# Channel-norm statistics: one instruction over two interleaved groups of 128 values

## The chip, the cores and the metric

The kernel runs on one core of a Trainium2 chip. The metric is the device time of one execution in microseconds (us), lower is better. Times of a kernel are compared by the median of several runs. The engines are PE (matmuls), PEld (its weight loads), DVE (VectorE), ACT (ScalarE), POOL (GpSimd) and SP (SyncE, which issues transfers here).

## The reference

The input is x of shape (4, 128, 128, 128): 4 images of 128 channels and 128 x 128 pixels, all float32. Two layers follow each other, each added to its input.

Layer 0 works on tokens, which are pixels with 128 channels. The input goes through a group norm, then through this block:

```python
t = _ln(t, ln0_g, ln0_b)
y1 = _ln(t, ln1_g, ln1_b)
att = jnp.einsum('btc,oc->bto', jax.nn.sigmoid(y1) * y1, W_out)
t = t + att
y2 = _ln(t, ln2_g, ln2_b)
wht = jnp.einsum('btc,oc->bto', y2, W_whiten)
k = jnp.square(jax.nn.relu(jnp.einsum('btc,hc->bth', wht, W_key)))
kv = jnp.einsum('bth,ch->btc', k, W_value)
r = jax.nn.sigmoid(jnp.einsum('btc,oc->bto', wht, W_recep))
t = t + r * kv
```

`_ln` subtracts the mean over the 128 channels of a token and multiplies by 1/sqrt(variance + 1e-5). The reference runs the block also on the transposed image and adds both, which is twice the same, as the block treats each token by itself.

Layer 1 is a group norm, a 3 x 3 convolution of 128 to 128 channels, a bias and a gate per channel.

The three calls of `_ln` are the channel norms that this change is about.

## The kernel before, in words

**Tiling.** An image is cut into 16 pairs of two halves. A half is 512 tokens, that is SUB = 4 groups of 128 tokens. So there are 64 pairs over the four images. PE transposes a half (`ut`, line L659) so that 128 tokens lie on the partitions and the channels in a row; a half is then a tile of 128 partitions x 4 groups x 128 channels.

**A norm of a pair.** For norm k (0, 1 or 2) and pair g, the following steps are made:

- `bn` (L690): for each half, four DVE instructions, one for each group. Each reads 128 contiguous values of every partition and writes six numbers. The instruction keeps the elements at even places and those at odd places apart: for each of the two it gives a count, a mean and a sum of squared deviations. So a token's 128 channels come out as two halves of 64, which have to be joined. Norm 0 reads `ut` in PSUM; norms 1 and 2 read `t` in SBUF.
- `norm_start` (L707 to L713): joins the two sets for the pair's 8 groups at once, on tiles of 128 x 8: the difference of the means, its square, a scaling with epsilon added, the sum of the two spreads, the total, and (norms 0 and 1) the sum of the means.
- `norm_root` (L718): the power -1/2 on POOL.
- `norm_end` (L724, L725), norms 0 and 1 only: halves the sum of means (with its sign turned) and multiplies it by the root, which gives the bias of the normalisation.

For the first two pairs (EARLY) `norm_start` and `norm_end` run on DVE, for all others on POOL.

**Who uses it.** Norms 0 and 1: ACT applies scale and bias (L666), eight instructions for a pair. After norm 0 POOL multiplies by the gain (L742) and adds the shift (L746). After norm 1 PE transposes back, ACT makes the SiLU (L757), PE multiplies by W_out (`att`, L763), and DVE adds the result to `t` (L767). Norm 2: DVE transposes the four rows of the tile `four` (L775), of which only the first is used; SP writes it to memory (L781) and reads it back spread over all partitions as `R` (L786), and DVE multiplies the transposed `t` by it (L799). This is the input of the key matmuls (`pk`, L810), whose results go through ACT (L814, L820) into the value matmuls (`kv`, L837). DVE and POOL add the outcome to the image (L847, L853, L857), and DVE takes statistics of it for layer 1 (L863). DVE also reads the images to come for their group norm (L1004).

**The convolution** of an image runs beside layer 0 of the next ones: DVE prepares sums of rows (L899 to L937), PE multiplies (`m`, L875 to L877), ACT and DVE put the rows together (L951 to L973).

**Order.** Each engine works through its queue in order, and the order is written out by hand in lists (FILL, FIRST, HANDOVER, ORDER, BOUND, END), from which the program issues one step after the other. The change leaves the lists as they are.

Of the kernel before, what the change touches and what calls it, by code (L numbers as in the profile page):

```python
# [9 lines left out]
F32 = mybir.dt.float32  # L10
AF = mybir.ActivationFunctionType
ALU = mybir.AluOpType

P = 128
CH = 512
SUB = CH // P
# [3 lines left out]
LN_EPS = 1e-5  # L20
# [261 lines left out]
def conv_preact_kernel(  # L282
# [40 lines left out]
    nc = tc.nc  # L323
    B, C, H, W = x.shape
# [8 lines left out]
    N = PAIR * SUB  # L333
# [7 lines left out]
    small = ctx.enter_context(tc.tile_pool(name="small", bufs=4))  # L341
# [67 lines left out]
    nhalf = const.tile([P, N], F32, tag="nhalf", name="nhalf")  # L409
# [233 lines left out]
    S = {}  # L643
# [38 lines left out]
    def norm_source(k, g, h):  # L682
        return S["ut", g, h] if k == 0 else S["t", g][:, h]

    def bn(k, g, h):
        if ("st", k, g) not in S:
            S["st", k, g] = small.tile([P, N, 6], F32, tag=f"st{k}", name="st", bufs=2)
        st, src = S["st", k, g], norm_source(k, g, h)
        for s in range(SUB):
            nc.vector.bn_stats(st[:, h * SUB + s, :], src[:, s, :])  # L690

    def norm_start(k, g, eng):

        st = S.pop(("st", k, g))

        def term(name):
            return small.tile([P, N], F32, tag=f"{name}{k}", name=name, bufs=2)

        if k < 2:
            rs, nb, sm = term("rs"), term("nb"), term("sm")
            d, dd = rs, rs
        else:
            S["turn", g] = four = small.tile([P, 4, N], F32, tag="four", name="four", bufs=2)
            rs, nb, sm, dd, d = four[:, 0], None, four[:, 1], four[:, 2], four[:, 3]
        eng.tensor_tensor(d, st[:, :, 1], st[:, :, 4], ALU.subtract)  # L707
        eng.tensor_tensor(dd, d, d, ALU.mult)
        eng.tensor_scalar(dd, dd, C / 4, C * LN_EPS, ALU.mult, ALU.add)
        eng.tensor_tensor(sm, st[:, :, 2], st[:, :, 5], ALU.add)  # L710
        eng.tensor_tensor(rs, dd, sm, ALU.add)  # L711
        if k < 2:
            eng.tensor_tensor(sm, st[:, :, 1], st[:, :, 4], ALU.add)  # L713
        S["terms", k, g] = rs, nb, sm

    def norm_root(k, g):
        rs, _, _ = S["terms", k, g]
        nc.gpsimd.tensor_tensor(rs, rs, nhalf, ALU.pow)  # L718

    def norm_end(k, g, eng):  # L720
        rs, nb, sm = S.pop(("terms", k, g))
        S["norm", k, g] = rs, nb
        if k < 2:
            eng.tensor_tensor(sm, sm, nhalf, ALU.mult)  # L724
            eng.tensor_tensor(nb, sm, rs, ALU.mult)  # L725

    def norm_terms(k, g):
        if g < EARLY:
            norm_end(k, g, nc.vector)
        else:  # L730
            norm_start(k, g, nc.gpsimd)
            norm_root(k, g)
            norm_end(k, g, nc.gpsimd)
# [274 lines left out]
    def layer0_op(op, g):  # L1008
# [4 lines left out]
            "u": lambda: lay(g, *d),  # L1013
            "Tu": lambda: lay_turned(g, *d),
            "bn": lambda: bn(d[0], g, d[1]),
            "sa": lambda: norm_start(d[0], g, nc.vector),
            "pw": lambda: norm_root(d[0], g),
            "nb": lambda: norm_terms(d[0], g),
            "t": lambda: first_norm(g, *d),
# [166 lines left out]
```

## Time and profile before

| what | value |
|---|---|
| median of 3 runs | 1869.69 us (1868.83 to 1871.25) |
| span of the profiled execution | 1871.1 us |
| PE busy | 1806.3 us (97%) |
| DVE busy | 1348.0 us (72%) |
| ACT busy | 1269.8 us (68%) |
| POOL busy | 1164.7 us (62%) |
| statistics of the norms (L690) | 219.0 us from SBUF, 112.3 us from PSUM |
| roots on POOL (L718) | 215.4 us for norms 0 and 1, 105.0 us for norm 2 |

The page gives one time for the profiled execution, its span from the first to the last instruction; the times of the runs stand beside it in a list of their own. A group of instructions is told by line, engine, operation, what it writes and reads, how often, its busy time and the mean of one in ns, and by the idle time of the engine just before it with what ended most of it. Durations of successive DVE instructions overlap, so the busy time of a group is less than count times mean. The granted clock of PE was 0.996 on the mean.

### The profile page before, as it was taken

The page shows a single profiled execution, that of the slowest core. Times are in us where ns is not written, and L with a number is a line of the kernel's source. Part 1 is how long each engine was busy: PE and PEld are TensorE (multiplying, and loading weights), DVE is VectorE, ACT ScalarE, POOL GpSimd, SP SyncE. Part 2 cuts the span into 40 slices and gives each one's busy share as a digit, 9 for nine tenths or more (in the row PEclk, how much of TensorE's full clock was granted, in tenths as well). Part 3 has the DMA queues.
Part 4 walks back from the last instruction along what each step waited for, and adds up shares of the span by engine and source line. Part 5 has one row for each costly group of instructions (what it writes and reads, how often), then busy time and mean ns, then how long its engine had stood idle before and what let it go on. Part 6 is the DMA issues. An engine that isn't in the chain of part 4 may idle for free.

```text
span 1871.1 us, 21825 instructions
## 1 busy us (share of the span) xinstructions
PE 1806.3 (97%) x6096; PEld 942.6 (50%) x6096; DVE 1348.0 (72%) x3336; ACT 1269.8 (68%) x2493; POOL 1164.7 (62%) x1915
## 2 busy tenths in 40 slices
PE   3799999999999999999999999999999999999999
PEld 2555555555545555455455455455455555554443
DVE  6767766677677677777757677777766667676987
ACT  2889899898666776777667777677766777753000
POOL 2878888887366666886556666788555667641211
PEclk9899999999999999999999999999999999999999
DMA  5211112221212212222112212211201111111112
GB/s 219 89 46 57 46 49 96 73 71 58 71 59 85 91 68 103 84 87 96 42 68 91 77 50 77 75 63 68 81 12 68 68 57 68 50 39 45 52 68 90
DMA packets 46072, 133.57 MB, mean 71 GB/s; under 512 B 8679, under 2 KB 15102, under 8 KB 38014
## 3 DMA queue, kind: packets, MB, share of 16 engines
q1 hardware_dynamic: 45504, 131.77, 20.5%
q8 instruction: 49, 0.80, 0.2%
q14 instruction: 73, 0.60, 0.1%
q10 hardware_dynamic: 446, 0.40, 0.1%
HBM read 97.14 MB, written 35.00 MB: 71 GB/s over the span
## 4 chain that ended last, share of the span: by engine, by line
PE 84%; DVE 5%; POOL 5%; DMA 3%; ACT 2%; issue 1%; SPq 0%; DVEq 0%; POOLq 0%
PE kv L837 21%; PE pk L810 21%; PE m L875 8%; PE m L877 8%; PE m L876 8%; PE pr L828 5%; PE att L763 5%; PE tt L659 3%; PE ut L659 3%; PE z1t L659 3%; DMA x<-in_x 1%; POOL rs L718 1%; DMA R<-rd 1%; DVE st L690 1%; ACT t L666 1%
## 5 line engine op out<-in xcount | busy, mean ns | idle before, releaser
L810 PE MATMUL pk<-y,wk_s 128*128 128x512 f32 x1024 | 503.3, 594 | 1.6 <-ACT h L814 0.9
L837 PE MATMUL kv<-h,wv 128*128 128x512 f32 x1024 | 492.7, 593 | 0.0
L814 ACT ACTIVATE h<-pk,kbias 128x512 f32<-128x512 f32 x512 | 349.3, 687 | 188.1 <-PE pk L810 178.3
L857 POOL TENSOR_TENSOR x<-x,r 128x512 f32<-128x512 f32 x128 | 166.7, 1302 | 202.4 <-DVE r L853 193.2
L837 PEld LDWEIGHTS kv<-h,wv 128*128 128x128 f32 x1024 | 187.1, 190 | 201.9 <-issue 177.2
L820 ACT ACTIVATE h<-h 128x512 f32<-128x512 f32 x480 | 286.5, 629 | 3.4
L810 PEld LDWEIGHTS pk<-y,wk_s 128*128 128x128 f32 x1024 | 183.0, 191 | 185.2 <-issue 148.0
L666 ACT ACTIVATE t<-ut,nb,rs 128x128 f32<-128x128 f32 x512 | 191.4, 466 | 90.6 <-POOL nb L725 82.7
L690 DVE BATCH_NORM_STATS2 st<-t 128x6 f32<-128x128 f32 x1024 | 219.0, 278 | 30.5 <-POOL t L746 28.7
L666 ACT ACTIVATE z<-t,nb,rs 128x128 f32<-128x128 f32 x512 | 209.5, 489 | 17.5 <-POOL nb L725 17.1
L718 POOL TENSOR_TENSOR rs<-rs,nhalf 128x8 f32<-128x8 f32 x128 | 215.4, 1682 | 6.0 <-DVE rs L711 6.0
L742 POOL TENSOR_TENSOR t<-t,g 128x512 f32<-128x512 f32 x128 | 163.8, 1285 | 74.7 <-ACT t L666 74.3
L875 PE MATMUL m<-v,u 128*128 128x512 f32 x384 | 198.5, 598 | 10.4 <-DVE v L899 5.0
L877 PE MATMUL m<-v,u 128*128 128x508 f32 x384 | 195.7, 591 | 0.0
L876 PE MATMUL m<-v,u 128*128 128x508 f32 x384 | 195.5, 591 | 0.0
L746 POOL TENSOR_TENSOR t<-t,b 128x512 f32<-128x512 f32 x128 | 166.0, 1304 | 5.6
L853 DVE SCALAR_TENSOR_TENSOR r<-r,kv 128x512 f32<-128x512 f32 x128 | 87.0, 680 | 86.2 <-PE kv L837 83.4
L763 PEld LDWEIGHTS att<-wo,y 128*128 128x128 f32 x1024 | 131.9, 196 | 31.5 <-issue 22.4
L767 DVE TENSOR_TENSOR t<-att,t 128x512 f32<-128x512 f32 x128 | 87.7, 685 | 78.3 <-PE att L763 77.8
L690 DVE BATCH_NORM_STATS2 st<-ut 128x6 f32<-128x128 f32 x512 | 112.3, 283 | 40.4 <-PE ut L659 39.8
L763 PE MATMUL att<-wo,y 128*128 128x128 f32 x1024 | 138.0, 280 | 0.8 <-DVE t L767 0.4
L828 PE MATMUL pr<-y,wr_s 128*128 128x512 f32 x256 | 130.7, 594 | 0.9 <-DVE h L824 0.7
(164 smaller groups left out, 2491.2 us busy)
## 6 DMA issues: line engine op xcount, KB each, us to landing
R<-rd SPq DMA_DIRECT2D x128, 256.0 KB
x<-in_x SPq DMA_DIRECT2D x31, 1024.0 KB
out<-x SPq DMA_DIRECT2D x31, 1024.0 KB
xs<-in_x SPq DMA_DIRECT2D x48, 512.0 KB
rd<-rrow SPq DMA_DIRECT2D x256, 1.0 KB
u<-raw SPq DMA_DIRECT2D x18, 192.0 KB
raw<-u SPq DMA_DIRECT2D x6, 192.0 KB
x<-in_x SPq DMA_DIRECT2D x2, 512.0 KB
```

What stands on the lines that cost most here:

```text
L666: nc.scalar.activation(dst[:, s, :], src[:, s, :], AF.Identity, bias=nb[:, i : i + 1], scale=rs[:, i : i + 1],)
L690: nc.vector.bn_stats(st[:, h * SUB + s, :], src[:, s, :])
L718: nc.gpsimd.tensor_tensor(rs, rs, nhalf, ALU.pow)
L763: nc.tensor.matmul(att[:, ts(s, P)], y[:, ts(s, P)], wo, start=True, stop=True)
L810: nc.tensor.matmul(pk, wk_s[:, ts(j, P)], S["y2", g, h], start=True, stop=True)
L814: nc.scalar.activation(k, S["pk", g, h, j], AF.Relu, bias=kbias[:, j : j + 1])
L820: nc.scalar.activation(k, k, AF.Square)
L828: nc.tensor.matmul(pr, wr_s, S["y2", g, h], start=True, stop=True)
L837: nc.tensor.matmul(S["kv", g, h], wv[:, j, :], S.pop(("h", g, h, j)), start=(j == 0), stop=(j == NH - 1))
L875: nc.tensor.matmul(pc, u[:, 1], v, start=True, stop=False)
L876: nc.tensor.matmul(pc[:, :, 1:W], u[:, 0], v[:, :, 0 : W - 1], start=False, stop=False)
L877: nc.tensor.matmul(pc[:, :, 0 : W - 1], u[:, 2], v[:, :, 1:W], start=False, stop=True)
```

## The change

A statistics instruction now reads two groups of 128 in alternation: element 0 of the first group, element 0 of the second, element 1 of the first and so on. The elements at even places are then those of one group and the elements at odd places those of the other, so that the six numbers are the two groups' own count, mean and spread. A half takes two such instructions of 256 elements instead of four of 128. The joining goes: `norm_start` only adds epsilon to the spread and turns the sign of the mean, and `norm_end` is one product. For norm 2 the one operation of `norm_start` fills all four rows of `four`.

```diff
     def bn(k, g, h):
         if ("st", k, g) not in S:
-            S["st", k, g] = small.tile([P, N, 6], F32, tag=f"st{k}", name="st", bufs=2)
+            S["st", k, g] = small.tile([P, N, 3], F32, tag=f"st{k}", name="st", bufs=2)
         st, src = S["st", k, g], norm_source(k, g, h)
-        for s in range(SUB):
-            nc.vector.bn_stats(st[:, h * SUB + s, :], src[:, s, :])
+        for s in range(0, SUB, 2):
+            i = h * SUB + s
+            two = src[:, s : s + 2, :].rearrange("p s c -> p c s")
+            nc.vector.bn_stats(st[:, i : i + 2, :].rearrange("p n f -> p (n f)"), two)
...
         if k < 2:
-            rs, nb, sm = term("rs"), term("nb"), term("sm")
-            d, dd = rs, rs
+            rs, nb = term("rs"), term("nb")
+            eng.tensor_scalar(rs, spread, C * LN_EPS, None, ALU.add)
+            eng.tensor_scalar(nb, mean, -1.0, None, ALU.mult)
         else:
             S["turn", g] = four = small.tile([P, 4, N], F32, tag="four", name="four", bufs=2)
-            rs, nb, sm, dd, d = four[:, 0], None, four[:, 1], four[:, 2], four[:, 3]
-        eng.tensor_tensor(d, st[:, :, 1], st[:, :, 4], ALU.subtract)
-        eng.tensor_tensor(dd, d, d, ALU.mult)
-        eng.tensor_scalar(dd, dd, C / 4, C * LN_EPS, ALU.mult, ALU.add)
-        eng.tensor_tensor(sm, st[:, :, 2], st[:, :, 5], ALU.add)
-        eng.tensor_tensor(rs, dd, sm, ALU.add)
-        if k < 2:
-            eng.tensor_tensor(sm, st[:, :, 1], st[:, :, 4], ALU.add)
-        S["terms", k, g] = rs, nb, sm
+            rs, nb = four[:, 0], None
+            eng.tensor_scalar(
+                four, st[:, :, 2:3].rearrange("p n f -> p f n").to_broadcast([P, 4, N]),
+                C * LN_EPS, None, ALU.add,
+            )
+        S["terms", k, g] = rs, nb
...
         if k < 2:
-            eng.tensor_tensor(sm, sm, nhalf, ALU.mult)
-            eng.tensor_tensor(nb, sm, rs, ALU.mult)
+            eng.tensor_tensor(nb, nb, rs, ALU.mult)
```

More of the change, by code (lines that the diff above doesn't have):

```diff
@@ L686, in bn @@
         if ("st", k, g) not in S:
-            S["st", k, g] = small.tile([P, N, 6], F32, tag=f"st{k}", name="st", bufs=2)
+            S["st", k, g] = small.tile([P, N, 3], F32, tag=f"st{k}", name="st", bufs=2)
         st, src = S["st", k, g], norm_source(k, g, h)
-        for s in range(SUB):
-            nc.vector.bn_stats(st[:, h * SUB + s, :], src[:, s, :])
+        for s in range(0, SUB, 2):
+            i = h * SUB + s
+            two = src[:, s : s + 2, :].rearrange("p s c -> p c s")
+            nc.vector.bn_stats(st[:, i : i + 2, :].rearrange("p n f -> p (n f)"), two)
     def norm_start(k, g, eng):
         st = S.pop(("st", k, g))
+        mean, spread = st[:, :, 1], st[:, :, 2]
         def term(name):
@@ L701, in norm_start @@
         if k < 2:
-            rs, nb, sm = term("rs"), term("nb"), term("sm")
-            d, dd = rs, rs
+            rs, nb = term("rs"), term("nb")
+            eng.tensor_scalar(rs, spread, C * LN_EPS, None, ALU.add)
+            eng.tensor_scalar(nb, mean, -1.0, None, ALU.mult)
         else:
             S["turn", g] = four = small.tile([P, 4, N], F32, tag="four", name="four", bufs=2)
-            rs, nb, sm, dd, d = four[:, 0], None, four[:, 1], four[:, 2], four[:, 3]
-        eng.tensor_tensor(d, st[:, :, 1], st[:, :, 4], ALU.subtract)
-        eng.tensor_tensor(dd, d, d, ALU.mult)
-        eng.tensor_scalar(dd, dd, C / 4, C * LN_EPS, ALU.mult, ALU.add)
-        eng.tensor_tensor(sm, st[:, :, 2], st[:, :, 5], ALU.add)
-        eng.tensor_tensor(rs, dd, sm, ALU.add)
-        if k < 2:
-            eng.tensor_tensor(sm, st[:, :, 1], st[:, :, 4], ALU.add)
-        S["terms", k, g] = rs, nb, sm
+            rs, nb = four[:, 0], None
[4 more added lines that the diff above has]
+        S["terms", k, g] = rs, nb
     def norm_root(k, g):
-        rs, _, _ = S["terms", k, g]
+        rs, _ = S["terms", k, g]
         nc.gpsimd.tensor_tensor(rs, rs, nhalf, ALU.pow)
     def norm_end(k, g, eng):
-        rs, nb, sm = S.pop(("terms", k, g))
-        S["norm", k, g] = rs, nb
+        S["norm", k, g] = rs, nb = S.pop(("terms", k, g))
         if k < 2:
-            eng.tensor_tensor(sm, sm, nhalf, ALU.mult)
-            eng.tensor_tensor(nb, sm, rs, ALU.mult)
+            eng.tensor_tensor(nb, nb, rs, ALU.mult)
     def norm_terms(k, g):
```

## The prediction, made before the changed kernel ran

> **What bounds the kernel now.** I read the page's busy times and slices first: which engine is full, and when.
>
> ```profile
> PE 1806.3 (97%) x6096; PEld 942.6 (50%) x6096; DVE 1348.0 (72%) x3336; ACT 1269.8 (68%) x2493; POOL 1164.7 (62%) x1915
> ...
> PE   3799999999999999999999999999999999999999
> ...
> DVE  6767766677677677777757677777766667676987
> ...
> POOL 2878888887366666886556666788555667641211
> ```
>
> PE is busy from the third slice to the end, so all that a change of DVE or POOL can win is PE's idle time, 1871.1 - 1806.3 = 64.8 us. The windows of 50 us say where it lies.
>
> ```profile
> 0.00:50.00 50.00, 14.56 (x44) 9.74 (x44) 32.24 (x87) 12.63 (x31) 11.64 (x21) 1.00 0.58 214
> 50.00:100.00 50.00, 43.25 (x167) 27.29 (x168) 39.32 (x134) 43.23 (x95) 44.60 (x74) 0.90 0.25 74
> ...
> 750.00:800.00 50.00, 48.49 (x161) 24.58 (x160) 40.06 (x106) 35.56 (x74) 42.94 (x65) 1.00 0.26 85
> ```
>
> The columns after the length are busy PE, PEld, DVE, ACT, POOL. In the first 100 us PE is idle for 50 - 14.56 + 50 - 43.25 = 42.2 us. From 100 to 1700 it loses 13.5 us in all (sum over the 32 windows), and the other 9 us lie after 1700, where no norm is left. Of the 13.5 us, 8.9 lie in the eight windows in which DVE is busy 38.5 us or more (1.1 us each), 4.6 in the other 24 (0.2 us each). So DVE at 77% of a window is where PE begins to starve.
>
> The chain of waits in the start shows what holds PE there: statistics, then a row of small terms, then the root.
>
> ```profile
> 35.76 1.75 DVE st L690 x8
> ...
> 37.54 0.18 DVE rs L707
> ...
> 64.41 1.63 POOL four L718
> ```
>
> The groups give the instructions that the change touches:
>
> ```profile
> L690 DVE BATCH_NORM_STATS2 st<-t 128x6 f32<-128x128 f32 x1024 | 219.0, 278 | 30.5 <-POOL t L746 28.7
> ...
> L718 POOL TENSOR_TENSOR rs<-rs,nhalf 128x8 f32<-128x8 f32 x128 | 215.4, 1682 | 6.0 <-DVE rs L711 6.0
> ...
> L707 POOL TENSOR_TENSOR rs<-st 128x8 f32<-128x8 f32 x124 | 37.7, 304 | 145.7 <-DVE st L690 144.7
> ```
>
> **What the Trainium skill says.** "SBUF — State Buffer", section "Door 1: The DMA port swizzle", in its note on cachelines: SBUF has lines of 16 bytes, at least two hits on a line are needed for full bandwidth, and each access that goes to a new line pays; PSUM's lines are 8 bytes. "VectorE: DVE Perf Modes", section "Walkthrough: the 8-slice pipeline in each mode", says the contrary for the plain mode: one element a cycle at 0.96 GHz, "fp32, weird strides, PSUM operands — all work". The new instruction reads 4 bytes here and 4 bytes 512 bytes further on, in turn: every read goes to another line. The trace has one small witness, the early joins on DVE:
>
> ```profile
> L713 DVE TENSOR_TENSOR sm<-st 128x8 f32<-128x8 f32 x4 | 0.7, 172 | 0.1
> ...
> L711 DVE TENSOR_TENSOR rs<-rs,sm 128x8 f32<-128x8 f32 x4 | 0.7, 166 | 0.1
> ```
>
> Both add two 8-element operands; L713 reads them 24 bytes apart (each in a line of its own), L711 side by side. L713 takes 6 ns more; L708 and L725, side by side too, take 168. One lost cycle for each of 8 elements would be 8 ns, none would be 0. Six is nearer the penalty, but 8 elements are few and two operands were read at once. So the trace leans to the first page without settling it.
>
> **The change part by part.**
>
> *Statistics.* The instruction order of every engine stays as it was apart from what is removed and added. Two instructions of 128 elements become one of 256: 1536 become 768, in 64 pairs x 3 norms x 2 halves = 384 halves of two each. Prices come from the timeline:
>
> ```profile
> 55.23 0.68 DVE L1004 BATCH_NORM_STATS2 st<-xs 128x6 f32<-128x512 f32 x1
> 55.82 0.86 DVE L690 BATCH_NORM_STATS2 st<-t 128x6 f32<-128x128 f32 x4
> 56.59 0.68 DVE L1004 BATCH_NORM_STATS2 st<-xs 128x6 f32<-128x512 f32 x1
> ```
>
> From start to start, 512 elements take 0.59 us and four times 128 take 0.77 us: 1.04 ns an element and 0.06 us an instruction. A half in two instructions then takes 2 x (0.267 + 0.06) = 0.65 us at full rate, -0.12 us; at half rate 2 x (0.533 + 0.06) = 1.19 us, +0.42 us. Over 384 halves DVE gains 46 us or loses 161 us. These are the two ends of the unknown price (a loss beyond half rate has nothing for it in the trace). I take half rate, for the note and the 6 ns.
>
> *Joining on POOL.* For each of 124 norms (the first two kinds) L707 to L713 and L724 go, 304 + 218 + 297 + 284 + 281 + 260 + 229 = 1873 ns by their means, and two scalar operations come, at L709's 297: -1.28 us. For 62 norms of the third kind 372 + 219 + 202 + 243 + 213 = 1249 ns become one operation on 32 elements (unseen; between L709's 202 and 400 ns, I take 300): -0.95 us. POOL falls by 159 + 59 = 218 us, to about 947 us. Nearly all of it is beside other work, since PE is full; it counts where POOL's row stands in the chain while PE is idle. The root (1.6 us) stays.
>
> *The first 100 us.* On the chain stand six norms. Their joins ahead of the root shrink: 0.87 to 0.2 (37.54), 1.09 to 0.2 (46.75), 0.87 to 0.2 (48.85), 1.04 to 0.4 (58.08), 2.0 to 1.2 (62.41, where 1.0 us looks like a held first instruction and stays), and POOL's at 68.50 by 1.3: -5.0 us. Statistics on this chain total 9.1 us, some 10.75 halves: -1.3 us at full rate, +4.5 us at half rate. Together -6.3 or -0.5 us. Next in line at full rate are DVE's waits for the read of the next image (2.1 us at 69.67), so I count three quarters, -4.7 us.
>
> *From 100 to 1700 us, at half rate.* The 359 halves there add 151 us to a DVE that is busy 1136 of 1600 us (71%, then 80%). Added to each window (a quarter of its L690 count x 0.42), 22 windows instead of 8 are at 38.5 us or more. At 1.1 us for those and 0.2 for the other 10, PE loses 26 instead of 13.5: +13 us. Queued behind the longer statistics on DVE are the sum with attention (L767), the key input (L799) and the conv's operands (L899), and PE waits for each of them. POOL's shorter rows give back about 3 us: a norm's latency changes by 2 x 0.42 - 1.28, a small gain. Bounds: if all of DVE's extra is hidden, 0 and the 3 us gained; if a quarter of the 151 us reaches PE, +38.
>
> *Sum.* The page gives one span, 1871.1 us, and the three listed times are 1868.8, 1869.7 and 1871.3, so next to nothing lies around the span; it stands 1.4 us above the median, and I take the differences from the median: 1869.7 - 0.5 + 13 - 3 = 1879 us. Own range of this case: 1866 to 1897.
>
> **The rivals.** *Faster, because alternating reads run at full rate.* Then DVE and POOL both get shorter, the order of each queue is unchanged, and nothing comes later. The start gives 4.7 us, and of the 13.5 us perhaps 8, those that follow a row of small POOL terms or DVE's fullest stretches: 1869.7 - 12.7 = 1857 us, at best -6.3 - 13.5, 1850. It speaks for it that 512 contiguous elements lose nothing at their line changes; against it the 6 ns. The point that decides is one number: a half breaks even on DVE at 0.77 us, thus at 1.22 cycles an element.
>
> *Hidden either way.* The penalty holds for one memory only (a third of the instructions read PSUM, two thirds SBUF), or DVE's idle 29% takes all of it while the start gains 2 to 4 us and POOL gives 3: 1864 to 1872, I say 1868. PE's 97% speaks for it; PE's sensitivity where DVE is over 77% speaks against.
>
> *The change doesn't do what it says.* The built program has 768 fewer statistics instructions and 868 fewer on POOL, with all others in their old order, so I give this nothing.
>
> **How the numbers follow.** Half rate with stalls 0.54, full rate 0.27, hidden or mixed 0.19. By 0.2% of the time, about what a measurement of this kernel can tell from no change (1866.0 to 1873.4), faster is 0.27 + 0.06 of the mixed + 0.02 of the first, 0.35; same is 0.10 of the mixed and 0.07 of the first, 0.17; slower is 0.45 + 0.03, 0.48. The likeliest case gives 1879 us. Since cases of both signs are left, the range goes from 1855, well into the full-rate case, to 1895.
>
> **What would show it.** In the new trace: the 128x256 statistics at about 680 ns each (0.59 from start to start) against 410 (0.33); PSUM and SBUF rows apart; DVE near 1500 us busy against 1300; POOL near 950; the first block of four key matmuls at about 76 us against 71; idle PE from 100 to 1700 near 25 us against 5, with waits for DVE first. The forecast is wrong if the statistics run at one element a cycle, or if they run at half and PE still never waits for them.

## The result and the profile after

| | median of the runs, us | lowest to highest |
|---|---|---|
| before, beside the change | 1870.47 (4 runs) | 1868.83 to 1872.19 |
| after | 1855.38 (4 runs) | 1854.62 to 1858.43 |

The ratio is 0.9925, with an interval of [0.9911, 0.9939]: the change saves 15 us. The prediction was 1879 us with a range of 1855 to 1895, on the other side of the kernel before. The measured time lies 0.4 us inside the lower end of that range, which was set so low for a rival. The profiled execution of after took 1858.43 us, the longest of its four, and its span is 1856.7 us, 14.4 us under that of before. The line numbers of after are two higher at the statistics (L692) and three lower from there on (the convolution's L875 is L872, the key matmuls' L810 is L807).

Busy times and slices of the kernel after:

```profile
PE 1801.5 (97%) x6096; PEld 944.4 (51%) x6096; DVE 1308.8 (70%) x2540; ACT 1271.1 (68%) x2493; POOL 989.1 (53%) x1047
...
PE   3899999999999999999999999999999999999999
...
DVE  6766666676667667877667667877766666666987
...
POOL 2867677775355555765435555666445556531111
```

DVE lost 39 us and POOL 176 us. PE's busy time also fell, by 4.8 us, for the same 6096 records: some of its matmuls had taken longer before. The windows of after (busy PE, PEld, DVE, ACT, POOL, then granted clock):

```profile
0.00:50.00 50.00, 15.79 (x48) 10.51 (x48) 31.30 (x66) 15.37 (x40) 14.22 (x22) 1.00 0.58 216
50.00:100.00 50.00, 47.42 (x191) 29.84 (x192) 35.98 (x84) 45.10 (x96) 43.77 (x51) 0.93 0.24 73
...
750.00:800.00 50.00, 50.00 (x175) 26.41 (x174) 40.31 (x77) 35.65 (x73) 32.24 (x32) 1.00 0.26 85
```

PE's idle time in the first 100 us fell from 42.2 to 36.8 us. Summed over the 32 windows from 100 to 1700 it fell from 13.5 to 9.1 us. So of the 14.4 us, 5.4 come from the start, 4.4 from idle time later, and 4.8 from matmuls that take less time; after 1700 PE idles 0.2 us more. The first key matmul starts at 70.42 us, in before at 76.29.

The groups of after that the change touched:

```profile
L692 DVE BATCH_NORM_STATS2 st<-t 128x6 f32<-128x256 f32 x512 | 189.8, 418 | 9.5 <-POOL t L743 7.6
L692 DVE BATCH_NORM_STATS2 st<-ut 128x6 f32<-128x256 f32 x256 | 96.3, 420 | 41.0 <-PE ut L659 37.9
...
L717 POOL TENSOR_TENSOR rs<-rs,nhalf 128x8 f32<-128x8 f32 x128 | 226.4, 1769 | 4.3 <-DVE nb L705 4.1
```

A statistics instruction of 256 alternating elements takes 418 ns from SBUF and 420 from PSUM as the mean of one, where the prediction named 680 for half rate and 410 for full rate. The timeline of DVE in after gives the price of a half from start to start:

```profile
52.78 0.75 DVE L692 BATCH_NORM_STATS2 st<-t 128x6 f32<-128x256 f32 x2
53.44 0.68 DVE L1001 BATCH_NORM_STATS2 st<-xs 128x6 f32<-128x512 f32 x1
```

53.44 - 52.78 = 0.66 us, against 0.77 before. The statistics run at full rate.

### The profile page after: what moved, and what is told of

The parts are those of the page before. It is cut to its first block, busy times and chain, and to the rows that moved or that the text cites. A ratio compares the mean times of both kernels' runs of the same rounds, so it can differ in the third digit from the quotient of the medians.

```text
span 1856.7 us, 20165 instructions
## 1 busy us (share of the span) xinstructions
PE 1801.5 (97%) x6096; PEld 944.4 (51%) x6096; DVE 1308.8 (70%) x2540; ACT 1271.1 (68%) x2493; POOL 989.1 (53%) x1047
## 4 chain that ended last, share of the span: by engine, by line
PE 89%; DVE 3%; DMA 1%; ACT 1%; POOL 1%; issue 0%; SPq 0%; DVEq 0%; POOLq 0%
PE kv L834 22%; PE pk L807 22%; PE m L872 9%; PE m L873 9%; PE m L874 8%; PE att L760 6%; PE pr L825 6%; PE tt L659 3%; PE z1t L659 3%; PE ut L659 3%; DMA R<-rd 1%; DMA rd<-rrow 1%; DVE v L896 0%; DVE u L606 0%; SPq L778 0%
## 5 line engine op out<-in xcount | busy, mean ns | idle before, releaser
L807 PE MATMUL pk<-y,wk_s 128*128 128x512 f32 x1024 | 502.1, 593 | 2.2 <-DVE y L796 1.2
L807 PEld LDWEIGHTS pk<-y,wk_s 128*128 128x128 f32 x1024 | 183.7, 190 | 183.1 <-issue 153.7
L717 POOL TENSOR_TENSOR rs<-rs,nhalf 128x8 f32<-128x8 f32 x128 | 226.4, 1769 | 4.3 <-DVE nb L705 4.1
L666 ACT ACTIVATE t<-ut,nb,rs 128x128 f32<-128x128 f32 x512 | 191.3, 466 | 37.0 <-POOL nb L722 31.2
L666 ACT ACTIVATE z<-t,nb,rs 128x128 f32<-128x128 f32 x512 | 209.3, 491 | 0.0
L872 PE MATMUL m<-v,u 128*128 128x512 f32 x384 | 198.0, 597 | 8.1 <-DVE v L896 4.1
L692 DVE BATCH_NORM_STATS2 st<-t 128x6 f32<-128x256 f32 x512 | 189.8, 418 | 9.5 <-POOL t L743 7.6
L704 POOL TENSOR_SCALAR rs<-st 128x8 f32<-128x8 f32 x124 | 41.9, 338 | 209.3 <-DVE st L692 208.0
```

Source lines behind the costliest of these rows:

```text
L666: nc.scalar.activation(dst[:, s, :], src[:, s, :], AF.Identity, bias=nb[:, i : i + 1], scale=rs[:, i : i + 1],)
L692: nc.vector.bn_stats(st[:, i : i + 2, :].rearrange("p n f -> p (n f)"), two)
L807: nc.tensor.matmul(pk, wk_s[:, ts(j, P)], S["y2", g, h], start=True, stop=True)
L872: nc.tensor.matmul(pc, u[:, 1], v, start=True, stop=False)
```

## The experiments

Diffs are against after or before, as each says. A time beside a ratio is a median; ratios are to the kernel before, run on the same chip, with their intervals. "Stall time" below is worked out from the trace: for each PE matmul, the time until the next one starts, less the median of that for its kind, summed where it is over 20 ns. It counts idle time and slow matmuls together. Each kernel has one trace, so small differences of stall time mean little (after and the kernel of the first experiment, which take the same time, have 15.8 and 12.6 us of it between 100 and 1690). For before it is 79.7 us, 47.0 of it in the first 100 us and 26.1 between 100 and 1690; for after 65.7, 41.4 and 15.8.

**Is the price the order of reading?** Against after, two contiguous groups are read in one instruction, so that the statistics mix two groups of tokens:

```diff
-            two = src[:, s : s + 2, :].rearrange("p s c -> p c s")
+            two = src[:, s : s + 2, :].rearrange("p s c -> p (s c)")
```

> The change with the two groups read one after the other in place of in alternation (the six numbers then mix both groups, so the norms are not the reference's). If alternating reads cost nothing, the 128x256 rows stay within 5 ns of 418 and 420 ns and the time within 2 us of the change, about 1855. If they cost a fraction of a cycle (rival: the 6 ns that the strided small join showed is a real price for each element), the rows get shorter by 20 ns or more and the time by 2 us or more.

Measured: 1855.32 us, 0.9911 [0.9899, 0.9924]; DVE busy 1305.3 us against 1308.8; the rows take 413 ns from SBUF and 421 from PSUM. Alternation costs nothing that can be seen in the time.

**The price by itself.** Against after, rows of eight equal DVE instructions are added at the end of the program, which was executed once. The last column counts them.

```diff
+        for i in range(8):
+            nc.vector.bn_stats(six_[:, i], two_.rearrange("p s c -> p (s c)"))
+        for i in range(8):
+            nc.vector.bn_stats(six_[:, i], two_.rearrange("p s c -> p c s"))
...
+        for i in range(8):
+            nc.vector.bn_stats(six_[:, i], spaced_[:, 0])
```

> The change with rows of DVE instructions behind the last work, eight of each: statistics of 256 elements contiguous, in alternation 512 bytes apart from SBUF and from PSUM, and of 128 elements 16 bytes apart; sums of two operands of 8 and of 128 elements, contiguous and strided; copies of 128 contiguous and strided. If strides cost nothing in SBUF and PSUM: equal times from start to start in each set, apart from the copy. If a new line costs a part of a cycle (rival): strided sets longer in proportion to the elements, 128-element sums by 16 times what 8-element sums show (6 ns, so about 90 ns).

The timeline of DVE in this run:

```profile
1852.28 2.70 DVE L1152 BATCH_NORM_STATS2 probe<-wk_s 128x6 f32<-128x256 f32 x8
1854.89 2.73 DVE L1154 BATCH_NORM_STATS2 probe<-wk_s 128x6 f32<-128x256 f32 x8
1857.54 2.73 DVE L1156 BATCH_NORM_STATS2 probe<-pprobe 128x6 f32<-128x256 f32 x8
1860.18 2.35 DVE L1158 BATCH_NORM_STATS2 probe<-wk_s 128x6 f32<-128x128 f32 x8
1862.45 0.69 DVE L1160 TENSOR_TENSOR probe<-wk_s 128x8 f32<-128x8 f32 x8
1863.06 0.74 DVE L1162 TENSOR_TENSOR probe<-wk_s 128x8 f32<-128x8 f32 x8
1863.71 1.70 DVE L1164 TENSOR_TENSOR probe<-wk_s 128x128 f32<-128x128 f32 x8
1865.33 2.42 DVE L1166 TENSOR_TENSOR probe<-wk_s 128x128 f32<-128x128 f32 x8
```

The rows are: 256 contiguous, 256 alternating between two runs 512 bytes apart, the same from PSUM, 128 elements 16 bytes apart; sums of 8 side by side, 8 at 24 bytes, 128 side by side, 128 at 16 bytes. The distances between starts, divided by eight, give 326, 331 and 330 ns for the first three: alternation is free in both memories. But a stride of 16 bytes is not: 284 ns for 128 elements, where a contiguous statistics instruction of before takes 0.77 / 4 = 0.19 us, and 294 against 202 ns for the sum, some 0.7 ns an element. The sum of 8 elements shows the same kind of price as the prediction's 6 ns (81 against 76 ns). The reads that pay use each stretch of 16 bytes once; in the change each is used four times, with another one in between. That this is the reason is not shown: no stride between the two was run.

**What if half rate had been true?** Against after, each of the 768 instructions reads the whole half of 512 elements, so that its statistics are those of four groups:

```diff
-            two = src[:, s : s + 2, :].rearrange("p s c -> p c s")
+            two = src.rearrange("p s c -> p (s c)")
```

> The change with statistics that take as long as the prediction had supposed: each of the 768 instructions reads all 512 elements of its half (the statistics are then of the whole half and not the reference's), 0.59 us from start to start. If the prediction's second step holds (PE loses 1.1 us in each window with DVE at 38.5 us or more), 1873 to 1883, slower than before. If DVE's idle time takes it (rival), 1856 to 1864, since the short joins remain.

The page of this run:

```profile
PE 1801.6 (97%) x6096; PEld 944.8 (51%) x6096; DVE 1496.6 (80%) x2540; ACT 1271.5 (68%) x2493; POOL 995.4 (53%) x1047
```

and its window of 750 to 800 us:

```profile
750.00:800.00 50.00, 50.00 (x175) 26.30 (x174) 46.83 (x82) 35.52 (x71) 34.46 (x35) 1.00 0.28 92
```

Measured: 1862.84 us, 0.9954 [0.9942, 0.9966], still faster than before. DVE is busy for 149 us more than before, and in 23 of the 32 windows for 38.5 us or more (the prediction had 22). Yet PE idles only 9.5 us from 100 to 1700. In the window shown DVE is at 94% and PE isn't idle at all. So the second step of the forecast fails as well: a DVE filled with statistics is not what starves PE.

**The two halves of the change.** Against after, the statistics alternate, but as many small instructions as the joins had are kept on POOL, some of them with no use:

```diff
+            eng.tensor_tensor(sm, mean, spread, ALU.subtract)
+            eng.tensor_tensor(sm, sm, sm, ALU.mult)
+            eng.tensor_tensor(sm, sm, spread, ALU.add)
...
+            eng.tensor_tensor(sm, mean, spread, ALU.add)
```

> The alternating statistics of the change, but with the row of small operations beside the root kept as long as before (seven on GpSimd for norms 0 and 1 ahead of the root or behind it, five for norm 2; their results are not used). If the gain of 15 us comes from the short row of joins (theory J), this kernel keeps only what DVE saves: about 1 us in the first 100 us and perhaps 1 us later, 1867 to 1870. If it comes from DVE's shorter statistics (theory S), it keeps most: 1856 to 1861.

Measured: 1860.52 us, 0.9939 [0.9927, 0.9951]. And against after, four instructions of 128 for a half as before, whose even channels alone are used, with the joins out:

```diff
-        for s in range(0, SUB, 2):
...
+        for s in range(SUB):
+            nc.vector.bn_stats(st[:, h * SUB + s, :], src[:, s, :])
```

> Four statistics instructions of 128 for each half as before, but the joins are left out: mean and spread are those of the 64 even channels alone, so that this part of the norms is not the reference's. Theory J: 1856 to 1861. Theory S: 1866 to 1870.

Measured: 1857.64 us, 0.9925 [0.9913, 0.9937]. Stall time in the start: 44.9 us with the statistics alone, 41.3 with the joins out, 41.4 with both; from 100 to 1690: 14.7, 14.8 and 15.8. The start's gain is that of the joins. Each theory is borne out by one of the two runs, so neither is the whole cause: later either part alone takes nearly the whole of the gain, and the gains don't add up.

**Where in time.** The change for the first four pairs only (g < 4), and for the others only (g >= 4); elsewhere the code of before runs:

```diff
+    def alternate(g):
+        return g < 4
...
```

> The change for the first four pairs alone (norms that lie in the first 100 us), the code of before for the other 60. The trace of the change has its first common landmark 5.9 us earlier, 1.05 us of that by an earlier load. If the start is worth what the chain says, 4.8 us, and nothing of it is lost later: 1865 to 1866 against 1870. If a gain at the start is given back at a later wait (rival): within 2 us of before.

> The reverse: the code of before for the first four pairs, the change for the other 60. By the stalls of PE after 100 us (about 8.5 us fewer in the trace of the change) 1860 to 1863; with the kernel of the first four pairs the two differences add up to about 15 us. Rival: the start is nearly all, then this one is within 3 us of before.

Measured: 1865.12 us, 0.9972 [0.9965, 0.9979], and 1862.07 us, 0.9953 [0.9937, 0.9968]. 5.0 and 8.1 us make 13 of 15: start and rest nearly add up. Stall time agrees: the first lowers the start's to 41.4 and leaves 24 later, the second leaves the start at 46.8 and 15.5 later.

**Which norm.** The change for norm 2 only (k == 2), and for norms 0 and 1 only (k < 2):

```diff
+    def alternate(k):
+        return k == 2
...
```

> The change for norm 2 alone (statistics alternating, no joins); norms 0 and 1 as before. If what delays PE is the row from the last statistics of a pair to the key matmuls, this keeps most of the gain after 100 us (8 us) and a part of the start's (1 to 2 of 5): 1859 to 1861. If it is POOL's long rows of norms 0 and 1: 1867 to 1870.

> The change for norms 0 and 1 alone; norm 2 as before. If POOL's long rows of norms 0 and 1 are the cause, this keeps nearly the whole gain: 1855 to 1859. If norm 2 is: the start's 3 to 4 us alone, 1866. If the stalls clear at any shift: 1857 to 1860 and the run with norm 2 alone is near 1861 too, so that the two gains together exceed that of the change.

Measured: norm 2 1865.34 us, 0.9978 [0.9972, 0.9985]; norms 0 and 1 1856.45 us, 0.9928 [0.9914, 0.9941]. Norms 0 and 1 alone give 13.1 us, nearly all. Norm 2 alone gives 4.2 us, between its two forecasts: it leaves the rows of norms 0 and 1 as they were, yet the stall time from 100 to 1690 us falls to 20.1. What norm 2's shorter row clears there was not followed.

**Shorter still, and moved to DVE.** Against after, the two scalar steps are made on DVE right behind the statistics (pairs from the third on):

```diff
+        S["seen", k, g] = S.get(("seen", k, g), 0) + 1
+        if g >= EARLY and S["seen", k, g] == PAIR:
+            norm_start(k, g, nc.vector)
...
-            norm_start(k, g, nc.gpsimd)
```

> The change, and the two small operations ahead of the root (norm 2: the one) made by DVE right behind the statistics instead of by GpSimd at the root's place. If the row on GpSimd ahead of the root is still what PE waits for after 100 us, 1 to 4 us faster than the change: 1851 to 1854. If the rest of PE's stalls are others (the spread of norm 2 through memory, the conv's sums on DVE), within 1 us of 1855, or slower by what DVE does more (rival).

Measured: 1854.93 us, 0.9918 [0.9902, 0.9935], not to be told from the change. ACT's wait for the bias at L666 falls from 28.9 to 13.9 us and nothing is won by it: after 100 us the row is short enough. The same edit was made on the kernel before, whose joins are six instructions:

> The statistics of before and the joins of before, but for pairs from the third on the joins ahead of the root are made on DVE right behind the statistics, not on POOL. DVE gains some 100 us of small instructions, POOL loses about 230 (1.7 ms for each 1000 norms). If POOL's row of small operations, each held behind others, is what delays the norms: most of the 8 us after 100 us and 1 to 2 us of the start come, 1860 to 1863. If the time that the norm's data takes through any engine counts, or DVE's load: 1868 to 1874.

Measured: 1877.49 us, 1.0044 [1.0032, 1.0057], slower; a miss. POOL fell to 914.4 us and DVE rose to 1524.8. On DVE, joins that wait for each other take about 0.2 us each from start to start, and PE's longest waits are for DVE then (L901, L959, L801, L826: 8.1 us in all). So the row was moved to the queue that PE's operands come from; that this is why it got slower is not shown. Why 1525 us of DVE cost here what 1497 didn't in the half-rate run was not separated further.

**One more statistics instruction.** Against before, the last instruction of a half is made twice:

```diff
+        nc.vector.bn_stats(st[:, h * SUB + SUB - 1, :], src[:, SUB - 1, :])
```

> The kernel before with one more statistics instruction in every half (the last is made twice, the result is the same): DVE +0.19 us a half, some +73 us in all, POOL as before. If the stalls after 100 us depend on the length of the path over the statistics (a knife's edge), they stay or grow and the start loses about 2 us: 1871 to 1878. If any shift of the instructions against each other clears them, as they vanished in every variant so far: 1862 to 1868.

Measured: 1890.64 us, 1.0113 [1.0099, 1.0127], more than either theory gave. DVE rose by 114 us, that is 0.30 us a half and not 0.19. Lengthening hurts, so it isn't that any shift clears the stalls. DVE has more to do as well, so this run alone doesn't tell length from load.

**Dose and place.** This leaves a threshold: how long ACT may wait for the bias of norms 0 and 1. On the changed kernel two, five and nine more small instructions were put on POOL ahead of the root, and for comparison five just behind the bias:

```diff
-            eng.tensor_scalar(nb, mean, -1.0, None, ALU.mult)
+            for _ in range(1 if g < EARLY else 1 + 5):
+                eng.tensor_scalar(nb, mean, -1.0, None, ALU.mult)
```

```diff
             eng.tensor_tensor(nb, nb, rs, ALU.mult)
+            for _ in range(0 if g < EARLY else 5):
+                eng.tensor_scalar(pad, rs, -1.0, None, ALU.mult)
```

> The changed kernel with the sign step of norms 0 and 1 made three times instead of once on POOL, ahead of the root (pairs from the third on; the result is the same): two more small instructions, some 0.55 us, in each of 124 rows. Threshold: the row stays 0.7 us under its length in the kernel before, so nearly nothing returns, 1855 to 1857. Load and holding by chance: a part returns in proportion to the instructions, 1858 to 1860.

> Five more small instructions ahead of the root, some 1.4 us a row, which with the 0.24 us that the statistics save is just under the length before. Threshold: near the edge, 1858 to 1866. Load: 1864 to 1868, the same as with the five behind.

> Nine more ahead of the root, some 2.5 us a row, about 1 us longer than before. Threshold: beyond the edge each 0.1 us of each norm reaches PE, well above the kernel before, 1885 to 1920. Load: 1870 to 1876.

> The changed kernel with five small instructions on POOL for each of the 124 norms, as in the run with five ahead, but just behind the bias, where ACT no longer waits for POOL. Threshold: as the change, 1855 to 1858, clearly under the run with five ahead. Load and holding by chance: the same as with five ahead, 1864 to 1868.

| kernel | row to the bias against before, us | time, us | ratio | stall time 100 to 1690, us |
|---|---|---|---|---|
| after | -1.4 | 1855.38 | 0.9925 [0.9911, 0.9939] | 15.8 |
| joins out alone | -1.2 | 1857.64 | 0.9925 [0.9913, 0.9937] | 14.8 |
| two ahead | -0.8 | 1856.59 | 0.9927 [0.9914, 0.9939] | 13.7 |
| statistics alone | -0.3 | 1860.52 | 0.9939 [0.9927, 0.9951] | 14.7 |
| half rate | -0.3 | 1862.84 | 0.9954 [0.9942, 0.9966] | 16.6 |
| before | 0 | 1870.28 | 1 | 26.1 |
| five ahead | +0.2 | 1868.49 | 0.9991 [0.9982, 1.0000] | 24.5 |
| one more statistics (on before) | +0.6 | 1890.64 | 1.0113 [1.0099, 1.0127] | 40.5 |
| nine ahead | +1.4 | 1953.09 | 1.0446 [1.0429, 1.0462] | 105.0 |
| five behind | -1.4 | 1861.83 | 0.9951 [0.9938, 0.9963] | 18.3 |

The second column is worked out from the traces. Its first part is POOL's row, from the first small instruction of norm 0 or 1 to the end of the bias, the shortest of 124: 3.64 us in before, 2.46 in after, 3.10, 4.05 and 5.30 with two, five and nine ahead, 3.51 with the statistics alone, 2.48 at half rate. Its second part is what the two halves' statistics take more or less than before: -0.22 us in the change, +0.82 at half rate, +0.6 with one more. The stall time is flat up to -0.3 us, higher from 0 on, and then rises ever more steeply: this is a threshold, with its edge between -0.3 and 0. Statistics alone and half rate lie on the flat part, though DVE is busy 1497 us in the second; what they lose against after lies mostly in the start, with 3.5 and 3.6 us more stall time. The times come from several chips, so the ratios are what to compare.

Of the four forecasts that with two ahead came true. Five ahead lies just above both of its ranges, nine ahead above both of its own, and five behind between the two. Five instructions cost 13 us ahead of the bias and 6.5 behind it (11.9 and 5.2 against the kernel with two ahead, timed on the same chip), with POOL at 1154 and 1142 us. So the place counts for half. The ones behind weren't free, as the threshold alone would have it: 1.8 us of their stall time fall in the start, some 1.2 us are matmuls that ran at half speed behind one idle time of 1.30 us, and what the rest waits for was not followed.

The waits of ACT from 100 to 1690 us (total, times, longest) say what stands still. Before:

```profile
ACT t L666 <- POOL nb L725: 78.0, 30, 5.2
```

after:

```profile
ACT t L666 <- POOL nb L722: 28.9, 26, 4.0
```

nine ahead:

```profile
ACT t L666 <- POOL nb L723: 143.7, 54, 6.9
```

and five behind, which is as after:

```profile
ACT t L666 <- POOL nb L724: 29.3, 26, 4.0
```

The sum of these waits is not what reaches PE: with the statistics alone ACT still waits 68.8 us here, and PE stalls no more than in after.

How such a wait reaches PE is seen in the chain of waits of before, at PE's longest stall after the start:

```profile
513.76 1.59 DVE st L690 x8
...
515.42 0.22 POOL rs L707
...
515.99 1.85 POOL rs L709
...
518.69 1.60 POOL rs L718
...
520.54 0.21 POOL nb L725
...
520.77 1.50 ACT t L666 x4
522.28 0.58 ACT h L814
522.86 0.59 ACT e L951
523.44 0.04 issue
523.49 0.70 PE m L875
```

ACT stands at the head of its queue, waiting for the bias (L666). Behind it is a row of the convolution (L951), which has nothing to do with the norm, but which PE needs to go on (L875). One of the joins, L709, is held: 1.85 us, where 0.20 is common. PE stalls for 2.07 us. The same place in after:

```profile
506.74 1.33 DVE st L692 x4
...
508.15 0.25 POOL rs L704
...
508.49 0.24 POOL nb L705
508.72 3.31 POOL rs L717
...
512.12 0.46 POOL nb L722
...
512.60 1.50 ACT t L666 x4
514.10 0.58 ACT h L811
514.68 0.59 ACT e L948
515.27 0.04 issue
515.31 0.70 PE m L872
```

Here the root itself is held, 3.31 instead of 1.6 us, and the stall is 0.92 us all the same. The row has become short enough to take up most of a hold. With the matmuls slowed behind them the two stalls make 4.0 and 1.2 us of stall time, a quarter of the difference between the traces after 100 us; the other stalls were not followed one by one. In the run with nine ahead, PE waits at this line, for ACT's L949, 13 times and for 19.7 us; in before once.

## Why the prediction was wrong, step by step

*Price of the statistics: wrong, the first step that failed.* "I take half rate, for the note and the 6 ns." Measured is 0.66 us a half, the full-rate 0.65 of the same text. The note of the Trainium skill in "SBUF — State Buffer", section "Door 1: The DMA port swizzle", says that each access to a new line pays; that holds here for a stride that uses a line once (0.7 ns an element), and not for two runs in alternation (331 against 326 ns). The 6 ns came from a stride of the first kind and were carried to the second. They could not be read from that trace either, because the early joins have a second sum that reads 24 bytes apart:

```profile
L710 DVE TENSOR_TENSOR sm<-st 128x8 f32<-128x8 f32 x4 | 0.7, 164 | 0.0
```

It takes 2 ns less than L711, which reads side by side. The Trainium skill's "VectorE: DVE Perf Modes", section "Walkthrough: the 8-slice pipeline in each mode", has one result a cycle for the plain mode. That holds for the change, and not for the stride of 16 bytes.

*Later stalls at half rate: wrong too, and apart from the first.* "At 1.1 us for those" windows of a full DVE PE was to lose 26 us. With half rate made true, 23 windows are so full and PE idles 9.5 us. PE's idle time and DVE's busy time lay in the same windows, but the one didn't follow from the other. Even with the price that it took, the forecast should have been below 1870: 1862.84 was measured. The term that was sized too small is the net length of the row, "2 x 0.42 - 1.28", valued at "a small gain" of 3 us. By the table above such a row, some 0.3 us shorter than before, already lies on the flat side of the threshold: 16.6 us of stall time against 26.1.

*What can be won: too narrow.* That "all that a change of DVE or POOL can win is PE's idle time" left out the matmuls that take longer around an idle time: 4.8 of the 14.4 us are PE's busy time.

*POOL: right in kind, a fifth too much.* 947 us were forecast, 989 measured, so it lost 176 us and not 218. By the busy times of their groups the small instructions fell by 206 of the 218 us (L709 takes 419 ns instead of the 300 assumed). The roots took 19 us back (1769 instead of 1682 ns for norms 0 and 1); the rest is not separated.

*First 100 us: right for full rate.* -4.7 us were forecast, -5.4 measured; the joins alone give -5.7 of stall time there, as against the -5.0 on the chain. For half rate it was -0.5, and the half-rate run has 1.9 us less stall time there than before.

*The rival, full rate: right.* It gave 1857 us, of which 8 us later "that follow a row of small POOL terms or DVE's fullest stretches". It is 9.2, 4.4 of idle time and 4.8 of matmuls that take less time, which the rival did not count; that its sum of 1857 is so close is in part luck. The first half of its reason is shown: the row to the bias of norms 0 and 1. The second is not.

*What stays open.* Why the edge is so sharp was not followed: the statistics alone shorten the row by 0.35 us and clear 11 us of later stalls, as much as the whole change does. The old joins on DVE (1877.49 us) and the five instructions behind the bias do not fit a threshold of this row alone.

## What to carry to other kernels

A wait at the head of an in-order queue holds up everything behind it: look for what stands behind the waiting instruction, not for how busy the engine is that it waits for. How much a row may grow or shrink is found by dose, a few small instructions ahead of the waited-for result and the same ones behind it. A price of a few ns seen on one pattern of addresses says nothing of another until that one is measured by itself: eight instructions in a row were enough here. A difference of a few ns between rows of a page is first held against other rows of the same kind.

## What the runs showed of the hardware

Small POOL instructions are held at times for as long as a root: 1.85 us instead of 0.20 for a join, 3.31 instead of 1.6 for a root. Their means (300 ns) hide it. DVE in before, beside the join that is held from 515.99 to 517.84 us:

```profile
515.86 0.73 DVE L899 SCALAR_TENSOR_TENSOR v<-p,mg,q 128x512 f32<-128x512 f32 x1
516.51 0.68 DVE L913 TENSOR_TENSOR q<-x 128x512 f32<-128x512 f32 x1
517.11 0.68 DVE L911 TENSOR_TENSOR p<-x 128x512 f32<-128x512 f32 x1
517.71 0.68 DVE L767 TENSOR_TENSOR t<-att,t 128x512 f32<-128x512 f32 x1
```

The join comes free when the last of three sums of rows for the convolution ends, at 517.79, although DVE works on. This is the rule in the trace: in before 163 of 1495 small POOL instructions take over 0.3 us more than the median of their line. Counted back from its end by that median, each of the 163 comes free within 0.15 us of the end of a DVE instruction that reads SBUF alone, most of them sums for the convolution, and none at the end of a statistics instruction or of one that reads PSUM. The half-rate run has 188 us more of statistics on DVE than after, and 74 of 565 small instructions are held, as against 73. So statistics don't hold POOL; that the sums do is what the times say, and no run took them away.

PE's stall of 2.07 us in before costs more than itself. The timeline and the window of before just after it:

```profile
523.49 1.13 PE L875 MATMUL m<-v,u 128*128 128x512 f32 x2 [2.07 <-ACT e L951]
524.45 1.69 PE L876 MATMUL m<-v,u 128*128 128x508 f32 x2
```

```profile
523.00:528.00 5.00, 4.51 (x7) 2.02 (x8) 1.77 (x3) 2.54 (x7) 4.54 (x8) 0.67 0.00 0
```

Two matmuls take 1.69 us, where two take 1.01 elsewhere, and the granted clock of these 5 us is 0.67. Some four matmuls run at half speed, 1.7 us more. After the stall of 0.92 us in after, the clock of the next 5 us is 1.00.

The length of the idle time alone doesn't decide it. Near 1710 us in after, PE idles 1.89 us at L558 and the clock is 0.66 for the next 5 us. The same wait in before is as long, and no matmul behind it is slowed:

```profile
1726.21 0.38 PE L558 MATMUL pm<-mv,gmat 128*128 128x1 f32 x2 [1.90 <-DVE mv L555]
1726.46 1.10 PE L875 MATMUL m<-v,u 128*128 128x512 f32 x2
```

All 18 traces have this wait, and in 9 of them the slow clock follows. Of the 29 idle times of PE over 1.85 us after the first 100 us of each trace, 15 are followed by it; of the 136 between 0.8 and 1.85 us one is. So a stall of about 2 us costs its own length or some 1.7 us more, and two traces of one program can differ by that. What decides between the two was not found.
